# The token-mixing sums of a fused transformer block, moved from VectorE to ScalarE and GpSimd

## The chip, the cores and the metric

The kernel runs on one core of one Trainium2 chip. The metric is the device time of one execution in microseconds (us). The engines are named as in the profile: PE (TensorE, matmuls), PEld (its weight loads), DVE (VectorE), ACT (ScalarE), POOL (GpSimd), SP (SyncE, here the issuer of most DMAs).

## The reference

The input x has 16 batches of 256 tokens and 256 channels, all in fp32. One block of a network is computed for each batch:

```python
x = x + time_mix(norm_mod(attention(x, mask), cond))     # first half
x = x + ffn_fp4(rotate(x))                               # second half
```

- `attention` has 16 heads of 16 channels, a mask over keys, and an output projection. Its result is normalized by its root mean square, multiplied by a gain and shifted; gain and shift come from the batch's conditioning vector.
- `time_mix` shifts half of the channels by one token (`xx`), and makes three mixtures, which are what this change is about:

```python
xk = x * mix_k + xx * (1.0 - mix_k)      # and xv, xr with mix_v, mix_r
k, v, r = xk @ Wk.T, xv @ Wv.T, xr @ Wr.T
out = (sigmoid(r) * wkv_scan(decay, first, k, v)) @ Wo.T
```

Here x stands for the normalized, modulated attention output. Only the lower 128 channels are shifted, so only they need mixing; for the upper 128 channels xx equals x, and the three mixtures are all x itself.
- `rotate` is a rotation of the channels by quaternions. `ffn_fp4` is a gated feed-forward layer with 704 hidden units, whose inputs and weights are rounded to a 4-bit float format in blocks of 16.

## The kernel before

Channels lie on the 128 partitions (two halves of 128 channels), tokens along the free dimension. A batch is therefore a tile of 128 x 2 x 256. The work of a batch is cut into stages, each a Python generator that emits a few instructions for one or more engines and then yields:

- `ask` (a): the q, k and v projections; from batch 2 on, q and k are split in two parts on POOL (L698) and spread by DMA (SP)
- `attend` (t): scores (L771, L763 for the first two batches), exponentials on ACT (L781, tile `w`), `values` (L793), division
- `leave` (l), eight steps: the output projection, the sum of squares on ACT (L841), `rstd` on POOL (L847, L848), scaling (L851), transposes of the normalized rows into a PSUM bank called `pn` (L656), the shifted lower half `xx` (L863), the upper half `xh` (L871), and the `xx` parts of the three mixtures (L876, tiles `mx`)
- `mix` (m): the three mixtures of the lower half are finished on DVE (L888). Then the k, v and r projections with the weights `ak`, `av`, `ar` (all L632), exponentials (L905, L907, L931), scans and the division. Its last step is a product on POOL (L939)
- `rotate` (r): output projection `ao`, rotation (L965, in the last three batches L956), and the first quantization
- `hidden` (h, i for the two token halves): the gate and up projections (L1005, L1018), activation, quantization (L553 to L563)
- `turn_h` (d, e): transposes of the quantized rows (L608)
- `down` (f): the down projection (L1087, L1094; in the last three batches L1067, L1070) and the output DMA
- beside these, stages for loading and preparing weights, among them R (the rotation, whose POOL scalings are L463 and L468) and W, V (quantizing the weights, L536 to L544)

Nothing in the file decides the order at run time. The string `ORDER` lists 1852 steps by hand-written name and batch (m0 is the next step of `mix` for batch 0, tf of `attend` for batch 15), and the kernel runs through it, so that the instructions of a step are appended to each engine's queue. An engine runs its queue strictly in that order and waits at each instruction until its inputs are there and its output buffer is free. PE thus works on several batches in turn, which fills its waits. A second string, `BANKS`, gives the PSUM bank (0 to 7) for each bank request in that order.

In the part that is changed: the mixture tile of k, for instance, is `mx["k"]`. `leave` writes into it (1 - mix_k) * xx plus the shift of the own part, on ACT. `mix` then reads the own x out of the bank `pn`, multiplies it by the gain of k, and adds the tile, in one DVE instruction. The bank `pn` is thus held until the third of these DVE instructions is done.

Of the kernel before, what the change touches and what calls it, by code (L numbers as in the profile page):

```python
# [8 lines left out]
F32 = mybir.dt.float32  # L9
# [4 lines left out]
AF = mybir.ActivationFunctionType  # L14
ALU = mybir.AluOpType
# [3 lines left out]
P = 128  # L19
# [12 lines left out]
a2 R l0 a2 M W0 l0 V0 W0 W3 l0 W5 M A t1 W3 A t1 l0 W2 t1 T a3 R l0 l0 a2 m0 l0 a3 l1 A l1 W0 m0 m0 R W1 m0 m0  # L32
m0 m0 m0 a2 l1 a2 m0 l1 t2 W5 V0 R t2 t2 t2 a3 m0 V1 m0 m0 t2 t2 m0 W3 l1 t2 W3 m0 l1 m0 t2 t2 t2 t2 R t2 t2 t2
R m0 V0 t2 W0 W0 l1 m1 a3 W4 a3 a3 m0 V0 W3 l1 t2 m1 W3 a3 t2 t2 W2 W2 W0 A m1 m1 l2 A m1 m1 W4 l2 r0 m1 l2 m1
l2 r0 a4 a3 m1 m1 l2 l2 m1 V1 m1 l2 a3 W2 m1 a3 t3 m2 W2 m1 t3 m1 t3 r0 t3 t3 a4 m1 t3 t3 l2 m2 a5 m2 t3 t3 r0
a4 m2 t3 t3 a4 t3 m2 t3 m1 a4 r0 m2 t3 m2 t3 a4 r0 r0 t3 r1 m2 a4 t3 m2 r1 a5 t3 r0 r1 a4 r1 r0 m2 m2 r0 r1 V1
V1 m2 a4 m2 a5 l3 r1 m2 a4 l3 l3 r1 i0 a5 i0 m2 V1 t4 i0 a4 t4 V1 i0 V1 i0 h0 t4 i0 r1 i0 t4 h0 h0 a5 t4 h0 t4
t4 l3 m2 t4 t4 i0 r1 i0 t4 t4 t4 t4 l3 t4 V1 a5 h0 i0 l3 t4 m2 r1 a5 i0 a5 l3 t4 l3 m3 e0 h0 t4 m3 r2 m3 a5 a5
V1 m3 i0 i0 m3 t4 r2 m3 a6 m3 m3 a6 a5 m3 a5 m3 l4 m3 e0 m3 l4 a6 m3 m3 a6 h0 t5 i0 t5 t5 m3 i1 a6 t5 m3 t5 h0
t5 i1 l4 i1 l4 t5 i1 t5 t5 t5 r2 t5 m3 t5 i1 t5 a6 l4 t5 a6 i0 t5 r2 r2 a7 i1 t5 e0 t5 a6 i1 l4 h0 h1 l4 d0 h0  # L40
m4 t5 h1 r3 h0 e0 r2 h1 h1 l5 h0 r3 l4 a7 r2 a6 m4 h1 l5 l5 h0 m4 a6 i1 m4 l5 a6 h0 a7 m4 r2 a6 m4 h1 d0 a7 m4
i1 m4 t6 e1 i1 h1 h1 r2 i1 e1 t6 t6 a7 m4 i1 m4 r2 m4 t6 d1 m4 m4 t6 t6 m4 m4 t6 t6 d1 t6 i1 t6 l5 h0 h2 t6 i1
i1 a8 t6 m4 t6 d0 l5 l5 h2 t6 h2 a7 h2 e1 a7 m5 l5 i2 d0 r3 e1 a7 a7 a7 h2 r3 a7 i2 r3 t6 i2 m5 i2 a7 m4 f0 f0
i2 r3 r3 i2 i2 h2 h1 m5 h1 r4 h2 h1 h2 f0 f0 t7 t7 f0 r4 t6 t7 t7 a8 d2 m5 t7 h1 t7 d2 h1 r3 a8 h1 m5 r3 m5 t6
t7 m5 h1 m5 t6 i2 t7 a8 t7 d1 h2 t7 t7 t7 t7 h2 e2 d1 h2 a8 t7 l6 l6 h2 m5 a8 l6 a8 m5 m5 l6 t7 l6 r4 a8 m5 h2
m5 e2 m5 r3 r4 i2 r4 l6 a8 i2 h2 a8 l6 h2 f1 a8 i3 m5 i2 r4 i3 m6 i3 a8 l6 m5 r4 i2 m6 a9 f1 m5 m6 i3 f1 i2 t8
t8 t8 f1 i2 t7 t8 d2 f1 t8 t8 i2 r5 t7 t8 t7 r5 d2 a9 t8 t8 a9 t8 t8 i3 m6 a9 a9 m6 t8 t8 i3 m6 i3 aa a9 m6 t8
e2 l7 m6 l7 a9 m6 m6 i3 h3 m6 i3 a9 l7 m6 h3 h3 h3 i3 l7 i3 i3 t8 e3 h3 h3 m6 e2 a9 h3 m6 h3 h3 e3 a9 i3 a9 f2
m6 i3 r4 f2 f1 h3 f2 a9 t9 t8 i3 t9 r4 t9 m6 t9 h3 f0 f2 t9 t9 f2 m6 e3 h3 r6 h3 r4 t9 t8 r6 h3 t8 t9 e3 t9 l7
d3 t9 aa d3 r5 aa t9 l7 l7 l7 i4 i4 t9 i4 h3 r5 r5 m7 r5 m7 aa i4 t9 d3 aa m7 m7 r5 t9 h4 ab m7 l8 i4 m7 m7 i4  # L50
h4 l8 i4 aa aa m7 m7 h4 d3 h4 h4 i4 m7 aa aa e4 i4 h4 m7 m7 l8 m7 i4 l8 t9 f3 l8 m7 i4 l8 l8 h4 h4 m7 d4 m7 h4
m7 i4 aa aa h4 f2 m8 h4 f3 h4 l8 i4 m8 i4 m8 aa r7 d4 h4 f3 e4 r5 i4 f3 ta h4 ta t9 f3 ta r7 h4 ta d4 ab ta t9
r7 ta ab r7 ab r7 ac ta d4 t9 ta ta r7 r7 r6 ta r6 m8 ab ta ta ta m8 m8 e4 ta r6 ab m8 m8 e4 m8 ab ab r5 m8 l9
ab ab r5 h5 m8 f3 h5 m8 i5 r6 h5 r6 i5 h5 l9 i5 h5 m8 h5 i5 ta i5 h5 l9 h5 m8 ab l9 h5 m8 i5 ab i5 tb r6 h5 tb
tb h5 r6 i5 h5 ta tb tb r6 e5 h5 f4 ta f4 m8 h5 ta tb m8 tb tb e5 tb tb f4 f4 d5 tb l9 l9 f4 r8 i5 l9 h5 tb d5
d5 r8 l9 r8 ac m9 m9 m9 r8 m9 m9 la r7 i5 r8 la r8 m9 h6 ad i5 i5 d5 r7 la r8 ac i5 h6 h6 ac i5 tb m9 i5 la h6
m9 e5 r7 m9 e5 ac la ac tb h6 ac m9 r8 la m9 h6 h6 la ma m9 ac m9 i6 m9 i6 m9 i6 h6 la ac ac i7 i6 ma d6 i6 ac
ma i6 i7 i7 m9 m9 h7 i7 tb ac i7 i7 d6 i6 h7 f5 i7 f5 h7 h7 i6 tc f4 tc tc i7 f5 tb tc h7 f5 h7 h7 f5 r9 r9 h6
tb i6 tc ad h6 h7 i6 tc e6 ad h6 ad h6 h6 r8 i6 tb h6 ad tc e6 tc tc tc ma tc ma i6 ma tc r8 tc tc e7 e7 ma h7
h6 h7 tc ma r9 r9 ad h7 i6 ad i7 ma r9 i7 ad h7 i7 ma h7 i6 lb ad r9 h7 i7 h8 ma lb ma i7 i6 ad lb d6 h8 e6 lb  # L60
lb r9 d6 lb h8 e6 lb ad r9 ma i7 h8 ma h8 mb ma f6 ad h8 td h8 ma tc h8 td td h7 lb td mb td f6 tc mb td r9 td
ae tc ma td td f6 d7 td i7 td mb mb d7 td mb r9 f6 i8 f6 ra i8 mb mb i8 td ra td e7 td ra d8 i8 ae i8 mb ae ra
e7 ra i8 ae ra td i8 mb d7 ra td ae ae i9 i9 mb lc i8 i9 i9 mb i9 lc i8 i9 ae lc f6 i8 ae ra ae mb ae ae lc lc
mb td i8 h8 f5 d7 i9 f7 lc h8 i8 h9 mb mb lc ae h8 h9 lc mc h8 mc i8 f7 i8 h8 h9 mb f7 h8 h9 mc h9 d8 f7 f7 te
te i8 rb mc te h9 rb h9 mc h9 mc rb te te af e8 te rb ra rb mc mc rb ld ld ld rb mc te ld mc te te i9 e8 te ld
i9 mc h8 ld i9 ra mc rb ld af te af i9 mc mc h9 te i9 md te i9 mc i9 af h9 e8 i9 te ld rb te af e9 mc h9 rb md
e9 md af te af e9 d8 md te h9 mc md te md af C md ia af d8 ia h9 md md ha ia ia md e8 ha ia f8 f8 e9 ha ia md f8
md ha ia tf tf h9 tf d9 d9 f8 md md ha md ia tf af tf af rc ia f8 ha md tf ia ha ia rc tf tf tf ia tf rc tf ib
rc tf tf ib ib ha tf ib da ia tf rc h9 f7 da tf rc ib d9 ia ib ea le tf hb le ib le ea tf le ha hb ia rc hb ha
ea ib le ib ha hb ha d9 hb le ea ha le rc le eb ha lf me ib me f9 ib hb md me lf me me hb rc ib me ib me hb me  # L70
ib rc hb hb f9 db f9 ha hb da me f9 db lf rd hb me lf hb ib lf hc eb hb da f9 me me rd eb hc lf hc hc f8 rd hb
lf me mf hc fa rd hc rd fa lf fa me hc rd mf me rd f9 mf db mf db hc dc mf rd ic fa mf rd me fa ic ic ic mf ic
rd dc me hc eb ic re hc mf re mf ic fb ic re ic hc re ic ec mf hc fb fb ic re hc hc hc ic ec mf mf mf dc id dc
ic mf re ic mf re ic id id fb id ec mf ec id re fc re hd fb mf fc id id id hd rf id re hd hd rf ed hd rf he id
rf ed ie rf hd hd id ie fc ie rf hd rf id rf dd hd ie dd hd hd rf id rf id hd he he he id ed hd hd ie if fa if
if hd ed if dd ie he dd fd he ie fd ie if he fd ie ee ie ie fd ee he he if hf if de hf he he de ie ie if ef fb
ef if he hf ie ie he he if hf ff ee ee he if hf de de if fd fe hf hf if hf hf hf hf fe hf hf if hf fe fc C df if
fe hf df ef ef fc fc df df ff ff ff ff C ff fe C ff
"""


BANKS = """
0123456701 2345670512 3470512364 7130526471 0357264135 7260413574 2603475045 3751062475 1062437504 2635704260
3425601734 2015437205 4736024173 5641735026 4137520417 4520734152 6451723451 7452374213 5062143502 1346703124
6031276352 1620127430 6052743052 4763021475 6210521547 1023564237 5062375041 2630741256 0754160253 4172501672
5416071254 6721540732 6732015432 7163721543 7215640713 5762145302 6170327604 5171423064 5273014562 7410367451
0324537426 3415073621 5076231540 6357402617 3520465731 7047230416 5027341237 4560523174 3026134027 1324601257
0263417264 5172451706 4570164235 7140235712 6352023167 0251473561 2473061247 0563270146 5702465724 3647023574
6125476152 4316705416 0753640756 2473651023 4673570214 3657234673 0536217430 1353671462 5013453125 2320452052
1023424510 5103210  # L90
"""


# [1 line left out]
def kernel(  # L95
# [28 lines left out]
    nc = tc.nc  # L124
    B, S, E = x.shape
# [15 lines left out]
    wk = ctx.enter_context(tc.tile_pool(name="work", bufs=1))  # L141
# [12 lines left out]
    def ps():  # L154
        return bank("ps")
# [141 lines left out]
    gain_of = const.tile([P, 3, NB], F32, tag="gain_of", name="gain_of")  # L297
    shift_of = const.tile([P, 3, NB], F32, tag="shift_of", name="shift_of")
    rest_of = const.tile([P, 3], F32, tag="rest_of", name="rest_of")
# [364 lines left out]
    xTs, qks, oTs, xns, ys, x1s, xqs, hqs = {}, {}, {}, {}, {}, {}, {}, {}  # L664
# [168 lines left out]
    def leave(b):  # L833
# [21 lines left out]
        pn = ps()  # L855
        transpose_all(pn, rn_)
        yield
        xx = xx_lo[b % 2]
# [6 lines left out]
            )  # L865
        yield

        mx = {}
        xns[b] = (mx, pn)
        mx["h"] = wk.tile([P, S], F32, tag="xh", name="xh", bufs=2)  # L870
        nc.scalar.activation(  # L871
            mx["h"], pn[:, S : 2 * S], AF.Identity, bias=shift[:, 1, b : b + 1], scale=gain[:, 1, b : b + 1]
        )
        for i, nm in enumerate("kvr"):
            mx[nm] = wk.tile([P, S], F32, tag="mx" + nm, name="mx")
            nc.scalar.activation(  # L876
                mx[nm], xx, AF.Identity, bias=shift_of[:, i, b : b + 1], scale=rest_of[:, i : i + 1]
            )
            if i == 0:
                yield  # L880
        yield


    def mix(b):
        mx, pn = xns.pop(b)

        for i, nm in enumerate("kvr"):
            nc.vector.scalar_tensor_tensor(  # L888
                mx[nm], pn[:, 0:S], gain_of[:, i, b : b + 1], mx[nm], ALU.mult, ALU.add
            )  # L890
            yield
        ek = wk.tile([P, E2, S], F32, tag="ek", name="ek")
        sa, sb = a_sum[b % 2], b_sum[b % 2]
# [243 lines left out]
    def exact(b, mask_b, v_pad, sl):  # L1137
# [82 lines left out]
        nc.vector.tensor_mul(flat(oT), flat(un), pd)  # L1220
        oTs[b] = oT
        yield from leave(b)

    ok = nc.values_load(within, min_val=0, max_val=1)
# [52 lines left out]
```

## Time and profile before

| what | before |
|---|---|
| median of 3 runs | 644.36 us (644.35 to 644.53) |
| the profiled execution's own time | 643.86 us |
| its span, first to last instruction | 642.1 us |
| granted TensorE clock, mean | 0.998 |
| last matmul ends at | 635.5 us |
| DMA moved | 57.71 MB, 90 GB/s |

A row of the groups reads: line, engine, operation, output tile and input tiles, shapes, count, then the busy time in us, the mean ns of one, and the engine's idle time before them with what ended it. A row of a timeline reads: start in us, duration in us, engine, line, operation, tiles, count; an idle time of the engine before it stands in brackets with what ended it. For TensorE one matmul of fp32 data is recorded as two rows, and a busy time includes the time in its pipeline, so that two matmuls that follow each other overlap in the records.

### The profile page before, as it was taken

How to read it: one execution, taken by the hardware profiler on the slowest of the kernel's cores; microseconds unless marked ns; L12 is line 12 of the kernel's file. 1: busy time of each engine (PE TensorE's matmuls, PEld its weight loads, DVE VectorE, ACT ScalarE, POOL GpSimd, SP SyncE). 2: the span in 40 equal slices, each digit the busy share in tenths (PEclk: the TensorE clock that was granted, in tenths of full speed). 3: DMA queues.
4: the chain of work that ended last, by engine and by line, in shares of the span. 5: the costliest groups of instructions: out<-in, count | busy, mean ns of one | idle time of the engine just before them, and what ended most of it. 6: DMA issues, size and time to landing. Idle time of an engine off the chain costs nothing.

```text
span 642.1 us, 11016 instructions
## 1 busy us (share of the span) xinstructions
PE 632.5 (99%) x3808; PEld 451.4 (70%) x3808; DVE 575.8 (90%) x1178; ACT 389.5 (61%) x903; POOL 161.6 (25%) x214
## 2 busy tenths in 40 slices
PE   9999999999999999999999999999999999999995
PEld 7568877676766777767767667767776667776674
DVE  6997899888988887999999999999999999999993
ACT  3879793866866565666665646754684665432442
POOL 3353213230313212222122321313131122212221
PEclk9999999999999999999999999999999999999999
DMA  6643524333341425233330322304305100000011
GB/s 169 172 149 120 165 83 132 132 116 117 115 136 61 147 51 174 69 103 115 124 107 17 132 83 93 122 1 125 106 33 174 25 2 16 17 1 1 2 32 55
DMA packets 62847, 57.71 MB, mean 90 GB/s; under 512 B 36912, under 2 KB 40896, under 8 KB 62784
## 3 DMA queue, kind: packets, MB, share of 16 engines
q1 hardware_dynamic: 62416, 56.65, 29.1%
q8 instruction: 32, 0.52, 0.3%
q10 hardware_dynamic: 368, 0.28, 0.1%
q14 instruction: 31, 0.25, 0.1%
HBM read 38.03 MB, written 18.87 MB: 89 GB/s over the span
## 4 chain that ended last, share of the span: by engine, by line
PE 82%; DVE 12%; ACT 2%; issue 2%; DMA 1%; SPq 0%; POOL 0%; DVEq 0%
PE ps L632 24%; PE ps L1005 14%; PE ps L793 9%; PE ps L644 7%; PE ps L1087 7%; PE pss L771 5%; PE ps L1018 5%; PE ps L608 3%; PE ps L965 2%; PE pss L763 2%; DVE v L561 1%; DVE am L553 1%; PE ps L656 1%; DVE ps L1034 1%; DVE th L1032 1%
## 5 line engine op out<-in xcount | busy, mean ns | idle before, releaser
L781 ACT ACTIVATE w<-pss 128x512 f32<-128x512 f32 x256 | 133.3, 611 | 48.7 <-PE pss L771 44.7
L1005 PE MATMUL ps<-guT,xqT 128*128 128x512 f32 x256 | 117.9, 594 | 0.1
L563 POOL TENSOR_TENSOR hq<-v,am 128x192 f32<-128x192 f32 (+1 forms) x64 | 50.1, 786 | 197.1 <-DVE v L561 177.6
L1005 PEld LDWEIGHTS ps<-guT,xqT 128*128 128x128 f32 x256 | 47.1, 190 | 42.3 <-issue 37.3
L698 POOL TENSOR_TENSOR two<-two 128x512 f32<-128x512 f32 x28 | 35.7, 1275 | 119.8 <-ACT two L691 85.2
L793 PE MATMUL ps<-w,v_one 128*32 128x256 f32 x1024 | 62.7, 382 | 0.3
L558 ACT ACTIVATE m<-ps 128x192 bf16<-128x192 f32 (+1 forms) x64 | 29.8, 467 | 49.7 <-DVE ps L556 49.3
L1087 PE MATMUL ps<-hT,downT 128*128 128x256 f32 x260 | 59.5, 379 | 0.0
L1087 PEld LDWEIGHTS ps<-hT,downT 128*128 128x128 f32 x260 | 49.1, 190 | 9.8 <-issue 2.2
L1030 ACT ACTIVATE th<-ps 128x192 f32<-128x192 f32 (+1 forms) x64 | 29.7, 467 | 40.0 <-PE ps L1005 20.5
L936 DVE RECIPROCAL den<-den 128x512 f32<-128x512 f32 x16 | 53.4, 3337 | 0.1
L793 PEld LDWEIGHTS ps<-w,v_one 128*32 128x32 f32 x1024 | 31.9, 109 | 25.9 <-ACT w L781 5.5
L771 PEld LDWEIGHTS pss<-qT,kT 64*128 64x128 f32 x448 | 30.6, 185 | 22.8 <-issue 10.6
L1018 PE MATMUL ps<-guT,xqT 128*128 128x384 f32 x128 | 46.6, 488 | 0.0
L771 PE MATMUL pss<-qT,kT 64*128 64x256 f32 x448 | 42.0, 306 | 0.1
L561 DVE SCALAR_TENSOR_TENSOR v<-m,ps 128x192 f32<-128x192 bf16 (+1 forms) x64 | 33.3, 521 | 4.5 <-POOL hq L563 0.5
L560 DVE SCALAR_TENSOR_TENSOR ps<-m,ps 128x192 f32<-128x192 bf16 (+1 forms) x64 | 33.2, 519 | 4.0 <-ACT m L558 3.9
L556 DVE SCALAR_TENSOR_TENSOR ps<-ps,rs 128x192 f32<-128x192 f32 (+1 forms) x64 | 34.1, 533 | 2.2
L608 PE MATMUL ps<-ident,hq 128*128 128x128 f32 (+1 forms) x204 | 34.7, 282 | 1.2 <-POOL hq L563 1.2
L608 PEld LDWEIGHTS ps<-ident,hq 128*128 128x128 f32 (+1 forms) x204 | 22.5, 135 | 18.3 <-issue 7.5
L1032 DVE SCALAR_TENSOR_TENSOR th<-th,ps 128x192 f32<-128x192 f32 (+1 forms) x64 | 32.1, 506 | 3.0 <-ACT th L1030 2.9
L1034 DVE SCALAR_TENSOR_TENSOR ps<-th,ps 128x192 f32<-128x192 f32 (+1 forms) x64 | 33.2, 518 | 1.2 <-PE ps L1005 0.2
(203 smaller groups left out, 1340.8 us busy)
## 6 DMA issues: line engine op xcount, KB each, us to landing
kept<-two SPq DMA_DIRECT2D x28, 512.0 KB, 2.8
qT<-kept SPq DMA_DIRECT2D x112, 128.0 KB, 2.9
kT<-kept SPq DMA_DIRECT2D x112, 128.0 KB, 2.8
x_sb<-in_x_dram SPq DMA_DIRECT2D x64, 64.0 KB, 2.4
out_dram<-o_sb SPq DMA_DIRECT2D x52, 64.0 KB, 1.9
out_dram<-o_sb SPq DMA_DIRECT2D x6, 128.0 KB, 1.7
raw<-in_L_ffn_w_down_dram SPq DMA_DIRECT2D x2, 352.0 KB, 3.8
raw<-in_L_ffn_w_gate_dram SPq DMA_DIRECT2D x5, 128.0 KB, 3.2
```

The lines of the kernel that those rows point to most:

```text
L561: nc.vector.scalar_tensor_tensor(v, m, BASE, x, ALU.max, ALU.subtract)
L563: nc.gpsimd.tensor_tensor(blk(dst), blk(v), bc(am), ALU.mult)
L608: nc.tensor.transpose(pt[0:n, (k - k0) * P : (k - k0 + 1) * P], src[:, k * P : k * P + n], ident)
L632: nc.tensor.matmul(pool_tile[:, ot * n : (ot + 1) * n], w[:, ct, ot * P : (ot + 1) * P], src[ct], start=(ct == 0), stop=(ct == E2 - 1),)
L644: nc.tensor.matmul(pool_tile[:, tt * E : (tt + 1) * E], srcT[:, ct, tt * P : (tt + 1) * P], w[:, ct, :], start=(ct == 0), stop=(ct == E2 - 1),
L771: nc.tensor.matmul(quad[2 * s + r][:, i * S : (i + 1) * S], kT[rows_, 2 * r + i, g, ks], qT[rows_, 2 * r + i, g, :], start=True, stop=True,)
L781: nc.scalar.activation(w[kt][:, r].rearrange("p i q -> p (i q)"), quad[r], AF.Exp)
L793: nc.tensor.matmul(pu[32 * r : 32 * r + 32, i * S : (i + 1) * S], vo[:, kt, 8 * g + 2 * r + i, :], w[kt][:, r, i, :], start=(kt == 0), sto ...
L936: nc.vector.reciprocal(flat(den), flat(den))
L1005: nc.tensor.matmul(p_[:, 0:n], xqT[:, ct, tt * P : (tt + 1) * P], guT[:, ct, base : base + n], start=(ct == 0), stop=(ct == E2 - 1),)
L1018: nc.tensor.matmul(p_[:, 0 : 2 * n].rearrange("p (u f) -> p u f", u=2), xqT[:, ct, tt * P : (tt + 1) * P], guT[:, ct, :].rearrange("p (u f ...
L1087: nc.tensor.matmul(pdn[:, 0:S], downT[:, k, h * P : (h + 1) * P], hT[:, k, :], start=(k == 0), stop=False)
```

## The change

Three things are done. First, ACT now makes both parts of a mixture, each in a tile of its own: the own part (gain times `pn` plus shift) in a new tile `own`, of which there are two buffers for the three parts k, v and r; and the rest, (1 - mix) * xx, in `mx`, now without the shift. Second, the addition is done by POOL, from two tiles on the chip; DVE has no part in it, and `pn` is read by ACT alone. Third, the first 250 of the 1852 steps in `ORDER` stay, and all behind them are put in a new order, with a new `BANKS`. The steps themselves are the same ones, apart from what the first two points change in them. Two of the kernel's helper stages (the fallback behind the check at the end, which does not run here) use the same functions. From line 889 on, a line of the new file has a number one lower than in the old one.

```diff
@@ -32,62 +32,62 @@
 m0 m0 m0 a2 l1 a2 m0 l1 t2 W5 V0 R t2 t2 t2 a3 m0 V1 m0 m0 t2 t2 m0 W3 l1 t2 W3 m0 l1 m0 t2 t2 t2 t2 R t2 t2 t2
 R m0 V0 t2 W0 W0 l1 m1 a3 W4 a3 a3 m0 V0 W3 l1 t2 m1 W3 a3 t2 t2 W2 W2 W0 A m1 m1 l2 A m1 m1 W4 l2 r0 m1 l2 m1
-l2 r0 a4 a3 m1 m1 l2 l2 m1 V1 m1 l2 a3 W2 m1 a3 t3 m2 W2 m1 t3 m1 t3 r0 t3 t3 a4 m1 t3 t3 l2 m2 a5 m2 t3 t3 r0
...
+l2 r0 a4 a3 m1 m1 l2 l2 m1 l2 r0 m1 m2 m1 W2 r0 a3 r0 m1 l2 a3 t3 t3 t3 m2 m1 m2 m2 t3 m1 r0 a4 r0 m1 a5 r0 t3
...
@@ -865,29 +865,28 @@
-        mx = {}
-        xns[b] = (mx, pn)
+        mx, own = {}, {}
+        xns[b] = (mx, own)
         mx["h"] = wk.tile([P, S], F32, tag="xh", name="xh", bufs=2)
         nc.scalar.activation(
             mx["h"], pn[:, S : 2 * S], AF.Identity, bias=shift[:, 1, b : b + 1], scale=gain[:, 1, b : b + 1]
         )
         for i, nm in enumerate("kvr"):
+            own[nm] = wk.tile([P, S], F32, tag="own", name="own", bufs=2)
+            nc.scalar.activation(
+                own[nm], pn[:, 0:S], AF.Identity, bias=shift_of[:, i, b : b + 1], scale=gain_of[:, i, b : b + 1]
+            )
             mx[nm] = wk.tile([P, S], F32, tag="mx" + nm, name="mx")
-            nc.scalar.activation(
-                mx[nm], xx, AF.Identity, bias=shift_of[:, i, b : b + 1], scale=rest_of[:, i : i + 1]
-            )
+            nc.scalar.activation(mx[nm], xx, AF.Identity, scale=rest_of[:, i : i + 1])
             if i == 0:
                 yield
         yield


     def mix(b):
-        mx, pn = xns.pop(b)
-
-        for i, nm in enumerate("kvr"):
-            nc.vector.scalar_tensor_tensor(
-                mx[nm], pn[:, 0:S], gain_of[:, i, b : b + 1], mx[nm], ALU.mult, ALU.add
-            )
+        mx, own = xns.pop(b)
+        for nm in "kvr":
+            nc.gpsimd.tensor_tensor(mx[nm], own[nm], mx[nm], ALU.add)
             yield
```

## The prediction

> **What bounds the kernel now.** I read the page's busy times first, then the engines' table by stretches of 8 us, then the timelines of PE and ACT where that table shows an engine without a gap.
>
> ```profile
> PE 632.5 (99%) x3808; PEld 451.4 (70%) x3808; DVE 575.8 (90%) x1178; ACT 389.5 (61%) x903; POOL 161.6 (25%) x214
> ```
>
> PE is busy 99% of the span. A busy PE need not be at its pace, so I compared starts with starts. A projection of four matmuls recurs every 1.73 us, a `values` group of 16 (L793) every 1.86 us, four 128x512 records every 1.72 us. Taking each kind of group at its shortest repetition, all the matmuls need some 615 us; the delays over that pace are 15 us in the whole run. Of these about 9 us are the same 0.09 us again and again, where the array changes from full height to 64 rows or 32 columns (169 such changes in the order before, 170 in the order after). The rest of the span is a start of 6.5 us before the first projection and 6.6 us after the last matmul (635.5 us). So waits for data on PE come to about 5 us, and this is all that a relieved VectorE can give back. In the last quarter DVE is nearly as full as PE (57.6 of 60 us between 500 and 560), but PE does not stand there.
>
> Where does PE depend on ACT?
>
> ```profile
> core 0: us, PE busy (x) PEld busy (x) DVE busy (x) ACT busy (x) POOL busy (x), PEclk, DMA share, GB/s
> 44.00:52.00 8.00, 8.00 (x67) 6.38 (x66) 6.93 (x26) 6.81 (x16) 6.07 (x18) 1.00 0.52 174
> 52.00:60.00 8.00, 7.90 (x51) 6.33 (x53) 5.93 (x12) 8.00 (x22) 2.16 (x3) 1.00 0.49 159
> ```
>
> Between 52 and 60 us ACT is busy 8.00 of 8.00: it is the bound of that stretch. Its timeline:
>
> ```profile
> 48.64 0.56 ACT L871 ACTIVATE xh<-ps,shift,gain 128x256 f32<-128x256 f32 x1
> 49.10 1.57 ACT L876 ACTIVATE mx<-xx_lo,shift_of,rest_of 128x256 f32<-128x256 f32 x3
> 50.58 0.58 ACT L690 ACTIVATE two<-ps 128x512 fp32r<-128x512 f32 x1
> ...
> 56.40 4.03 ACT L781 ACTIVATE w<-pss 128x512 f32<-128x512 f32 x8
> 60.23 0.68 ACT L931 ACTIVATE ps<-ps 128x512 f32<-128x512 f32 x1
> ```
>
> No row from 48.64 to 60.75 has an idle time before it. The eight exponentials of `w` end at 60.4 us, and PE needs the last of them:
>
> ```profile
> 48.86 1.89 PE L644 MATMUL ps<-wt_o,oT 128*128 128x256 f32 x8
> 50.59 0.59 PE L632 MATMUL ps<-mx,wt_ak 128*128 128x256 f32 x2
> ...
> 59.90 2.06 PE L793 MATMUL ps<-w,v_one 128*32 128x256 f32 x32
> 61.89 0.74 PE L771 MATMUL pss<-qT,kT 64*128 64x256 f32 x8
> ...
> 68.00 1.93 PE L793 MATMUL ps<-w,v_one 128*32 128x256 f32 x32
> 69.86 0.66 PE L333 MATMUL ps<-ident,yT 128*128 128x128 f32 x4
> ```
>
> The `values` group at 59.90 takes 1.99 us to the next start, the one at 68.00 takes 1.86. The difference is PE waiting for ACT: there is no slack here. The first 250 steps of the order, which stay as they are, reach to about 78 us and hold the mixing of batches 0 and 1.
>
> **The change part by part.** The rows for its pieces:
>
> ```profile
> L888 DVE SCALAR_TENSOR_TENSOR mx<-ps,gain_of,mx 128x256 f32<-128x256 f32 x48 | 22.1, 471 | 4.4 <-ACT mx L876 4.3
> L871 ACT ACTIVATE xh<-ps,shift,gain 128x256 f32<-128x256 f32 x16 | 9.0, 564 | 0.4
> L698 POOL TENSOR_TENSOR two<-two 128x512 f32<-128x512 f32 x28 | 35.7, 1275 | 119.8 <-ACT two L691 85.2 <-issue 26.6 <-DVE rs L555 7.8
> ```
>
> DVE loses 48 instructions, 22.1 us: 576 becomes 554. ACT gains 48 reads of a PSUM bank, each like L871. From its start to the next start that one takes 0.46 us (48.64 to 49.10), so 48 x 0.46 = 22 us: 390 becomes 412. The other part stays (L876 recurs each 0.49 us; dropping its bias changes no size). POOL gains 48 adds of 128x256. The nearest row is L698, two full fp32 inputs of SBUF, 1.275 us for 512 columns. Half is 0.64; scaling the 128x256 multiply with a broadcast input (0.62 us) by 1275/1060, the two kinds at 512, gives 0.75. I take 0.70, so 34 us: 162 becomes 195, 30%.
>
> Against this stands the Trainium skill, GPSIMD Engine Reference, "Engine selection": elementwise work with two inputs belongs on VectorE, GpSimd being about twice as slow. The row agrees on the slowness (0.70 against 0.47), but by it POOL has 480 us free. By the rule each mix pays 0.23 us three times, 11 us in all, if the adds were on the path; by the rows they are not, as soon as the order leaves room. From the transposes of `pn` (L656) to the first `ak` matmul the new order has between 5.9 and 40 us of PE work in batches 1 to 15. The chain in between (shift 1.1, `xh` 0.5, own 0.5, rest 0.6, add 0.7: 3.4 us) fits. In batch 0 it is 3.5 us from the transposes' end to L632, and there it does not.
>
> Batch 0, worked out (with each engine's instructions in the new order): own k at 49.10, rest k 49.56 to 50.16, the add on POOL 50.2 to 50.9. On POOL the eight rotation scalings that used to run until 50.2 now stand behind the three adds; they end near 55.2 and are needed at 56.3, and `rstd` follows at 55.9, before ACT asks for it. PE asks for the k sum at 50.59 and gets it at 50.95: 0.4 us of wait. Own r reuses own k's buffer (two for three parts), so it waits for the k add, 50.95; ACT would reach it at 51.0, so this wait costs nothing here. L690 then starts at 52.0 in place of 50.58: ACT is 3 x 0.47 = 1.4 us late, has no idle time to absorb it, and the last exponential ends at 61.8. PE's `values` group, come at 60.3, goes on at 61.8, and the next group starts 1.2 to 1.4 us late; the 0.4 lies inside this. Bounds: 1.2, and 2.1 if the k add is held up. For that second bound: SBUF — State Buffer, "Who interferes with whom", says that a VectorE instruction with two SBUF inputs and a GpSimd read exclude each other. L540 and L541 (two SBUF inputs, 0.69 us each) stand at 50.1 here; no row has one beside an add. I take 1.3, since L888 no longer stands before them and they can run earlier.
>
> Batch 1: own k delays ACT by 0.46, with 0.15 us of idle before L690 at 67.69; own v and r add 0.95; the idle 0.68 before `ek` at 72.28 takes most of it. 0.6 us reaches `rnorm` at 74.01, and 0.2 of it the transposes at 77.27. Range 0 to 0.5. Together the kept prefix costs 1.5 us (1.2 to 2.6).
>
> Behind step 250 the order is new on every engine. Summing rows over the new order, DVE has 0 to 7 us less work per 100 us of PE, ACT 2 to 5 more (at most 75 of 100), POOL 3 to 7 more; DVE is again the fullest (97 of 100 from 300 to 400 us and after 500), and none exceeds PE. PE's own work and its mode changes are equal. What was waited for there is about 4 us, nearly 2 of it at the very end:
>
> ```profile
> 628.27 0.60 PE L608 MATMUL ps<-ident,hq 128*128 128x128 f32 x4
> 629.58 0.55 PE L608 MATMUL ps<-ident,hq 128*128 128x128 f32 x3 [0.70 <-POOL hq L563]
> 630.66 0.44 PE L608 MATMUL ps<-ident,hq 128*128 128x128 f32 x2 [0.54 <-POOL hq L563]
> ```
>
> PE waits there for the last hidden rows to come through DVE and POOL. Before: 3.0 us of down projection stands between the last L1018 and these transposes; in the new order 5.6 us. That can hide up to 1.7 us. On the other side, a new order brings new collisions: own r behind the k add in all 16 batches, with hq or yT multiplies that wait for DVE queued ahead on POOL in most of them, and behind own r on ACT the exponentials that PE needs. I set these against each other: -0.1. SP issues the same DMAs in a new order; they have slack before (no DMA holds PE after 6 us).
>
> **Sum.** Span 642.1 + 1.5 - 0.1 = 643.5. The profiled execution took 643.86, 1.8 more than its span, and the median of the runs is 644.36, 0.5 above that; 644.36 + 1.4 = 645.8.
>
> **The rivals.** (1) Prefix cost alone, as above: 645.8, 38%. (2) The end gives it back: the 2.6 us of extra cover take away the 1.7 us of waits, and the prefix costs 1.5: 644.2, no measurable change, 35%. For it: the longer cover; against: DVE is full before it, so the last rows may simply come later. (3) Faster, not slower: DVE's 22 us matter wherever PE waits for DVE or POOL; end -1.7, half of the 2 us of other waits -1, prefix at its least 1.2: 644.36 - 1.5 = 642.9. It decides if the exponentials at 56.4 start less than 1 us late. Since PE's waits are only 5 us in all, it can hardly give more; 15%. (4) The two-buffer ring: own r stands on ACT for the k add while POOL waits for DVE, 0.5 us in each of the 14 later batches where ACT then is late for `w`, tanh or abs: with half of it passed on to PE 3.5 us, 649.3, 12%. For it: POOL's queue waits for DVE 178 us in front of hq; against: ACT is at most 75% full there.
>
> 0.2% (1.3 us) is about what a measurement of this kernel tells from no change. Faster 15%, same 35%, slower 50%. The range 643.0 to 649.0 leaves out half of (3) and the upper half of (4); the likeliest case alone is 645.4 to 647.0.
>
> **What would show it.** After: L690 near 52.0, `values` near 60.3 with 3 us to the next start; ACT 8.00 of 8.00 there; own about 0.56 each, adds about 0.70; no change in PE's count; the waits at 628 shorter. Wrong if PE's starts at 62 us are where they were, or if PE shows stops of over 0.3 us between 100 and 600 us.

## The result, and the profile after

| | before | after |
|---|---|---|
| median, beside each other on one chip (19 runs each) | 644.53 us | 645.61 us |
| ratio to before, 95% interval | 1 | 1.0015 (1.0008 to 1.0022) |
| the same on a second chip (57 and 22 runs) | 645.90 us | 646.11 us; 1.0013 (1.0003 to 1.0023) |
| the profiled execution's own time, span | 643.86, 642.1 us | 645.88, 644.1 us |
| last matmul of any size starts at | 635.27 us | 637.26 us |

One of the 22 executions on the second chip (731.85 us, at a clock of 0.85) was in the slow state, and the ratio leaves it out. The kernel is about 1 us slower (0.5 to 1.4 us by the first interval, 0.2 to 1.5 by the second), just what a measurement can tell. First the page's busy times after:

```profile
PE 634.2 (98%) x3808; PEld 451.7 (70%) x3808; DVE 563.5 (87%) x1130; ACT 408.2 (63%) x951; POOL 195.8 (30%) x262
```

DVE fell from 575.8 to 563.5, ACT rose from 389.5 to 408.2, POOL from 161.6 to 195.8; PE's count did not change. The groups of the new instructions:

```profile
L889 POOL TENSOR_TENSOR mx<-own,mx 128x256 f32<-128x256 f32 x48 | 34.8, 728 | 45.8 <-ACT mx L880 44.8
L876 ACT ACTIVATE own<-ps,shift_of,gain_of 128x256 f32<-128x256 f32 x48 | 27.1, 564 | 1.6 <-POOL mx L889 1.6
L880 ACT ACTIVATE mx<-xx_lo,rest_of 128x256 f32<-128x256 f32 x48 | 24.4, 508 | 0.2 <-PE ps L632 0.2
```

The add takes 0.73 us and the own part 0.56. The rows show an idle time of 1.6 us in all before the own part, waiting for POOL. The stretch from 52 to 60 us in the table by stretches:

```profile
core 0: us, PE busy (x) PEld busy (x) DVE busy (x) ACT busy (x) POOL busy (x), PEclk, DMA share, GB/s
52.00:60.00 8.00, 7.56 (x42) 6.07 (x41) 4.08 (x8) 7.99 (x22) 5.33 (x13) 1.00 0.54 174
```

ACT is full, as before (the fourth busy time, 7.99 of 8), and POOL's 2.16 of 8 has become 5.33. The timelines of PE, ACT and POOL in this stretch:

```profile
44.69 1.93 PE L793 MATMUL ps<-w,v_one 128*32 128x256 f32 x32
...
51.26 0.70 PE L632 MATMUL ps<-mx,wt_ak 128*128 128x256 f32 x2 [0.16 <-POOL mx L889]
...
56.64 0.61 PE L771 MATMUL pss<-qT,kT 64*128 64x256 f32 x5
57.50 1.64 PE L771 MATMUL pss<-qT,kT 64*128 64x256 f32 x11 [0.25 <-ACT rnorm L851]
...
61.55 1.99 PE L793 MATMUL ps<-w,v_one 128*32 128x256 f32 x32
63.47 0.75 PE L771 MATMUL pss<-qT,kT 64*128 64x256 f32 x8
```

```profile
52.10 0.58 ACT L690 ACTIVATE two<-ps 128x512 fp32r<-128x512 f32 x1
...
55.71 0.89 ACT L748 ACTIVATE v_one<-ps,keep 128x256 f32<-128x256 f32 x2
56.61 0.84 ACT L851 ACTIVATE rnorm<-ps,rstd 128x256 f32<-128x256 f32 x2
```

```profile
50.48 1.57 POOL L889 TENSOR_TENSOR mx<-own,mx 128x256 f32<-128x256 f32 x2 [2.53 <-ACT mx L880]
52.28 0.72 POOL L889 TENSOR_TENSOR mx<-own,mx 128x256 f32<-128x256 f32 x1 [0.22 <-ACT mx L880]
...
55.11 0.37 POOL L468 TENSOR_SCALAR x1T<-ident,cols 64x64 f32<-64x64 f32 x1
55.57 0.22 POOL L847 TENSOR_SCALAR ms<-ms 128x2 f32<-128x2 f32 x1
55.87 0.71 POOL L848 TENSOR_TENSOR rstd<-ms,mhalf 128x2 f32<-128x2 f32 x1
```

The `values` group at 44.69 stood at 44.34 before, and nothing changed lies ahead of it: the first loads came a little later in this execution. Such shifts of the start, up to 2.8 us between two executions, enter before 12 us and are carried on to the end; this, more than the kernels, spreads the times. So from here on I measure from the start of this group: **A** to the next `values` group (batch 0), **T** to the start of the last matmul (L510). Before: A = 59.90 - 44.34 = 15.56, T = 635.27 - 44.34 = 590.93. After: A = 16.86, T = 592.57. So batch 0 costs 1.30, and everything behind it 0.34 in this execution (0.00 in a second one, below). At the end PE no longer waits (before, 0.70 and 0.54 us at these transposes):

```profile
626.29 2.76 PE L1066 MATMUL ps<-downT,hT 128*128 128x256 f32 x12
628.88 0.61 PE L1069 MATMUL ps<-ident,x1T 128*128 128x128 f32 x4
629.33 2.32 PE L1066 MATMUL ps<-downT,hT 128*128 128x256 f32 x10
631.49 1.38 PE L608 MATMUL ps<-ident,hq 128*128 128x128 f32 x9
```

### The profile page after: what moved, and what is told of

It reads as the page before. It is cut to its first block, busy times and chain, and to the rows that moved or that the text cites. A ratio compares the mean times of both kernels' runs of the same rounds, so it can differ in the third digit from the quotient of the medians.

```text
span 644.1 us, 11082 instructions
## 1 busy us (share of the span) xinstructions
PE 634.2 (98%) x3808; PEld 451.7 (70%) x3808; DVE 563.5 (87%) x1130; ACT 408.2 (63%) x951; POOL 195.8 (30%) x262
## 4 chain that ended last, share of the span: by engine, by line
PE 85%; DVE 9%; ACT 3%; issue 1%; POOL 1%; DMA 1%; SPq 0%; DVEq 0%; POOLq 0%
PE ps L632 23%; PE ps L1004 14%; PE ps L793 9%; PE ps L644 7%; PE ps L1086 7%; PE ps L1017 6%; PE pss L771 5%; PE ps L608 4%; PE ps L1066 2%; PE ps L964 2%; PE pss L763 2%; PE ps L656 1%; DVE den L935 1%; DVE v L561 1%; PE ps L1093 1%
## 5 line engine op out<-in xcount | busy, mean ns | idle before, releaser
L563 POOL TENSOR_TENSOR hq<-v,am 128x512 f32<-128x512 f32 (+1 forms) x64 | 50.1, 785 | 160.9 <-DVE v L561 149.2
L558 ACT ACTIVATE m<-ps 128x512 bf16<-128x512 f32 (+1 forms) x64 | 29.8, 466 | 60.7 <-DVE ps L556 60.6
L698 POOL TENSOR_TENSOR two<-two 128x512 f32<-128x512 f32 x28 | 35.6, 1271 | 86.9 <-ACT two L691 44.5
L1029 ACT ACTIVATE th<-ps 128x512 f32<-128x512 f32 (+1 forms) x64 | 29.6, 466 | 38.4 <-PE ps L1004 27.0
L889 POOL TENSOR_TENSOR mx<-own,mx 128x256 f32<-128x256 f32 x48 | 34.8, 728 | 45.8 <-ACT mx L880 44.8
L1031 DVE SCALAR_TENSOR_TENSOR th<-th,ps 128x512 f32<-128x512 f32 (+1 forms) x64 | 32.3, 507 | 10.5 <-ACT th L1029 10.5
L561 DVE SCALAR_TENSOR_TENSOR v<-m,ps 128x512 f32<-128x512 bf16 (+1 forms) x64 | 33.3, 521 | 4.6
L556 DVE SCALAR_TENSOR_TENSOR ps<-ps,rs 128x512 f32<-128x512 f32 (+1 forms) x64 | 34.1, 533 | 2.2
L560 DVE SCALAR_TENSOR_TENSOR ps<-m,ps 128x512 f32<-128x512 bf16 (+1 forms) x64 | 33.2, 518 | 3.1 <-ACT m L558 2.7
L1033 DVE SCALAR_TENSOR_TENSOR ps<-th,ps 128x512 f32<-128x512 f32 (+1 forms) x64 | 33.2, 519 | 2.9 <-PE ps L1004 1.7
```

The source lines that it names most:

```text
L561: nc.vector.scalar_tensor_tensor(v, m, BASE, x, ALU.max, ALU.subtract)
L563: nc.gpsimd.tensor_tensor(blk(dst), blk(v), bc(am), ALU.mult)
```

## The experiments

The theories: **1**, ACT, with three more instructions in batch 0 of the kept prefix, makes PE late there, and the new order behind step 250 nets about nothing. **Rival A** (not the interval A), the new order is the cost. **B**, DVE's relief is what pays later. **C**, the POOL add ahead of `ak` is the cost. **D**, the new instructions need the new order. The **ring** of two own tiles. Two were added for the end: E1 (the place of the last down projections gives back the waits there) and E2 (DVE's lighter load does). All twelve kernels, with A and T as above ("rest" is T - A, before 575.37) and the ratio to the kernel before on the same chip:

| kernel | A | rest | T against before | ratio, 95% interval |
|---|---|---|---|---|
| after, a second time | 16.87 | 575.37 | +1.31 | 1.0013 (1.0003 to 1.0023) |
| after, batches 0 and 1 mixed as before | 15.78 | 575.77 | +0.62 | 1.0012 (1.0000 to 1.0024) |
| before, 3 more ACT reads in batch 0 | 17.53 | 575.37 | +1.97 | 1.0035 (1.0023 to 1.0046) |
| new instructions, old order | 16.85 | 584.55 | +10.47 | 1.0163 (1.0140 to 1.0186) |
| after, all adds on DVE | 16.61 | 593.69 | +19.37 | 1.0289 (1.0263 to 1.0315) |
| after, three own tiles | 16.76 | 575.65 | +1.48 | 1.0016 (1.0007 to 1.0025) |
| after, batch 0's adds on DVE | 16.61 | 575.73 | +1.41 | 1.0025 (1.0015 to 1.0035) |
| after, 11 batches mixed as before | 15.79 | 598.38 | +23.24 | 1.0324 (1.0301 to 1.0346) |
| before, tail of the new order | 15.56 | 575.38 | +0.01 | 1.0001 (0.9993 to 1.0009) |
| after, tail of the old order | 16.85 | 575.40 | +1.32 | 1.0028 (1.0018 to 1.0037) |
| after, two copies on DVE | 17.21 | 575.48 | +1.76 | 1.0036 (1.0022 to 1.0049) |
| before, that tail and two copies on DVE | 15.57 | 575.02 | -0.34 | 0.9997 (0.9989 to 1.0006) |

The two profiled executions of the kernel after agree within 0.01 us in A and differ by 0.34 in the rest. Each row rests on one profiled execution; that of "11 batches" is the slowest of its five runs (671.41 us, median 667.10), so that its T is some 4 us above the usual.

**Batch 0: taking the change out of the prefix.**

```diff
+            if b < 2:
+                own[nm] = pn
...
```

The same test stands at the addition, which DVE makes from the bank where b < 2.

> The kernel after, in its order and with its banks, but batches 0 and 1 mixed as before (the own part read from the bank and added by DVE, ACT makes only the xx part). Theory 1 (three more ACT instructions in batch 0 of the kept prefix cost 1.2 us, the new order behind it about nothing): 1.2 us below the kernel after, 644.4, equal to the kernel before; L690 of batch 0 back at 50.6 to 51.0 us and no wait at the first L771 behind 57 us. Rival A (the new order behind step 250 costs it): equal to the kernel after, 645.6. Rival C (only the slower POOL add ahead of the first ak costs, 0.3 us): 645.3.

A falls by 1.08 to 15.78, of the 1.30 that it had gained; L690 is back at 51.00 and the score group is whole. So the cost lies in batch 0, in the size of theory 1, and rival A in its strict form falls. But the edit takes away ACT's own parts and POOL's adds at once, and does not tell these two apart. The last 0.2 stay open: PE's v projection starts 0.15 us late (at 52.88), and no wait shows why. T falls by 1.02 against the first execution of after and 0.69 against the second. The medians alone do not tell the two kernels apart.

**Batch 0: adding the ACT work to the kernel before.**

```diff
+            for _ in range(1 if b == 0 else 0):
+                own = wk.tile([P, S], F32, tag="own", name="own", bufs=2)
+                nc.scalar.activation(
+                    own, pn[:, 0:S], AF.Identity, bias=shift_of[:, i, b : b + 1], scale=gain_of[:, i, b : b + 1]
+                )
```

> The kernel before, with three more ACT instructions in batch 0 alone: the own part of each mixture is also written by ACT into a tile that nobody reads; DVE goes on mixing from the bank. Order and banks are those of before. Theory 1 (ACT has no slack from 49 to 60 us): 3 x 0.46 = 1.4 us later on ACT, 1.1 to 1.4 us longer, 645.7, with L690 near 52.0 us. Rival A (the new order costs it) and rival C (the POOL add costs it): as before, 644.5, no change over 0.2 us.

The two rows of ACT and PE that say most:

```profile
52.64 0.57 ACT L877 ACTIVATE own<-ps,shift_of,gain_of 128x256 f32<-128x256 f32 x1 [0.55 <-DVE mx L893]
```

```profile
55.66 1.99 PE L644 MATMUL ps<-wt_v,xT 128*128 128x256 f32 x8 [1.01 <-ACT two L691]
```

More than expected: +1.97. ACT's own v had to wait 0.55 us, because DVE reads the same bank here and the program makes the two readers take turns (DVE's next reading waited 0.25 us for ACT's own r, with which it shares only the bank). At L690 ACT is 2.02 us later than before, measured from the same landmark ((54.54 - 46.28) - (50.58 - 44.34)), and this becomes 1.97 on PE, and then nothing more to the end. So ACT's lateness is passed on nearly one to one, without POOL having any part in it.

**Batch 0: which engine?** In the first kernel here the three adds of batch 0 go to DVE and ACT keeps both parts; in the second, ACT is relieved of two copies (r weights, a part of the gate weights) and POOL keeps the adds.

```diff
-            nc.gpsimd.tensor_tensor(mx[nm], own[nm], mx[nm], ALU.add)
+            (nc.vector if b < 1 else nc.gpsimd).tensor_tensor(mx[nm], own[nm], mx[nm], ALU.add)
```

> The kernel after, but the three additions of batch 0 stand on DVE; ACT still makes both parts. Theory 1 (three more ACT instructions cost the 1.2 us in batch 0): as the kernel after within 0.4 us, with the values group still 1.2 us late against its pace. Rival C (the slower POOL add costs it): 0.4 to 1.2 us below the kernel after.

```diff
-            if name in ("q", "k", "v", "o"):
+            if name in ("q", "k", "v", "o", "ar"):
-        nc.scalar.copy(guT[...], pt[...])
+        copy = nc.vector.tensor_copy if j == 2 * P else nc.scalar.copy
+        copy(guT[...], pt[...])
```

> The kernel after with two copies out of a bank in batch 0's stretch (the weights of the r projection, and one quarter of the gate weights) moved from ACT to DVE, which stands idle for 2 us there. Theory 1 (ACT is the bound from 49 to 60 us, one to one): ACT is 0.94 us earlier there, and the interval from the values group at 44.6 us to the one at 61.5 falls from 16.86 to 15.9 to 16.0 us, the whole by 0.9 us, to the level of the kernel before. Rival C (POOL's add or another wait sets it): 16.6 or more.

With the adds on DVE, A is 16.61: ACT alone still costs 1.05, and POOL has 0.25 of the 1.30. With all 48 adds on DVE (below) A is 16.61 again. With ACT relieved, 15.9 to 16.0 was expected, and A rose to 17.21. Theory 1 in its simple form fails here. ACT's, POOL's and PE's timelines of that kernel:

```profile
51.49 0.56 ACT L877 ACTIVATE own<-ps,shift_of,gain_of 128x256 f32<-128x256 f32 x1 [0.34 <-POOL mx L890]
...
53.66 0.40 ACT L842 ACTIVATE rnorm<-ps 128x256 f32<-128x256 f32 x1
...
56.85 0.84 ACT L852 ACTIVATE rnorm<-ps,rstd 128x256 f32<-128x256 f32 x2 [0.75 <-POOL rstd L849]
```

```profile
50.38 1.76 POOL L890 TENSOR_TENSOR mx<-own,mx 128x256 f32<-128x256 f32 x2 [2.54 <-ACT mx L881]
52.52 0.73 POOL L890 TENSOR_TENSOR mx<-own,mx 128x256 f32<-128x256 f32 x1 [0.39 <-ACT mx L881]
...
55.36 0.37 POOL L468 TENSOR_SCALAR x1T<-ident,cols 64x64 f32<-64x64 f32 x1
55.81 0.22 POOL L848 TENSOR_SCALAR ms<-ms 128x2 f32<-128x2 f32 x1
56.11 0.71 POOL L849 TENSOR_TENSOR rstd<-ms,mhalf 128x2 f32<-128x2 f32 x1
```

```profile
51.51 0.70 PE L633 MATMUL ps<-mx,wt_ak 128*128 128x256 f32 x2 [0.51 <-POOL mx L890]
```

ACT is at the scaling (L852) early, and stands there 0.75 us for `rstd`, which POOL makes only behind three adds and eight rotation scalings. L852 starts 0.03 us after `rstd` ends (56.11 + 0.71 = 56.82, and 56.85). Look back at the rows of after: there `rstd` ends at 55.87 + 0.71 = 56.58, and ACT's scaling starts at 56.61, again 0.03 behind it. So POOL holds ACT up in the kernel after too, though no idle time stands in that row. By its own queue ACT would have come earlier. From the two `v_one` (L748) to the scaling it takes 0.73 us before and 0.71 with batch 0's adds on DVE, where `rstd` is there in time, as two ACT instructions overlap in the records; in after it takes 56.61 - 55.71 = 0.90. The rows of before, and of the kernel with batch 0's adds on DVE:

```profile
54.24 0.84 ACT L748 ACTIVATE v_one<-ps,keep 128x256 f32<-128x256 f32 x2
54.97 0.84 ACT L851 ACTIVATE rnorm<-ps,rstd 128x256 f32<-128x256 f32 x2
```

```profile
58.04 0.90 ACT L748 ACTIVATE v_one<-ps,keep 128x256 f32<-128x256 f32 x2
58.75 0.92 ACT L851 ACTIVATE rnorm<-ps,rstd 128x256 f32<-128x256 f32 x2
```

So batch 0 is late for two reasons that lie side by side. ACT's own parts alone make 1.05. POOL's adds, with ACT relieved, still make the whole delay, and in after they are the later of the two: `rstd` comes 0.18 behind ACT's own queue, and the k add, as the next run shows, holds own r up by 0.10. So taking away the adds alone gives 0.25, taking 0.94 off ACT alone gives nothing, and taking away both gives 1.08. That A even rose by 0.35 is the work of one slow k add (1.08 us, see the last section): by it own r waits 0.34 us, PE 0.51 in place of 0.16, and `rstd` ends 12.24 us behind the landmark in place of 11.89. Without it A would be about 16.86, an estimate from these rows.

**The ring of own tiles.**

```diff
-            own[nm] = wk.tile([P, S], F32, tag="own", name="own", bufs=2)
+            own[nm] = wk.tile([P, S], F32, tag="own", name="own", bufs=3)
```

> The kernel after with three buffers for the own tiles, so that own r need not wait for the k add (a small one-time tile of the test in batch 2 moves into that ring to make room). Theory 1 (this ring costs nothing, since own r waited once in 48): equal to the kernel after within 0.5 us. Ring rival: 1 us or more below the kernel after.

The kernel after beside it:

> The kernel after, unchanged, beside the next three on the same chip, so that they can be set against it directly. All theories: 1.0 to 1.2 us above the kernel before.

T differs by 0.17, and the ratios overlap nearly whole. But A, which repeats within 0.01, is 16.76 in place of 16.87: with two tiles own r starts 0.49 us behind the rest of v (50.75 to 51.24 in after), behind the k add, and with three 0.40. So the ring has 0.10 us of batch 0's cost, and nothing measurable of what lies behind it (575.65, between the two executions of after).

**Behind step 250: the new instructions in the old order.** The order and the banks are those of before, the code that of after. One of the five small moves:

```diff
-l3 m3
+m3 l3
```

> The new instructions (own part on ACT, add on POOL) in all batches, with the order and the banks of before; only in batches 3, 7, 9, 12 and 14 the last step of leave moves behind the k add, by 1 to 8 steps, since two own tiles serve three parts. Theory 1 (prefix +1.2, later batches have slack on ACT and POOL): 645.7 to 646.5, about the kernel after. Rival A (the new order itself is the cost): as before or faster, 644.5 or less. Rival D (the longer chain of own, rest and add stands right ahead of ak in the old order and needs the new order to be hidden): over 647, with waits of L632 for POOL's add in more than ten batches.

A is 16.85, exactly that of after; but the rest is 9.18 us longer. D holds, and theory 1's 645.7 to 646.5 does not, though D's waits were expected at the wrong place: the line of L632 waits for the add only 0.5 us. The largest stop, in the timelines of POOL, SP's DMA queue and PE, all of this kernel (its line numbers are one lower than those of after):

```profile
128.64 1.58 POOL L888 TENSOR_TENSOR mx<-own,mx 128x256 f32<-128x256 f32 x2 [5.91 <-ACT mx L879]
130.44 0.73 POOL L888 TENSOR_TENSOR mx<-own,mx 128x256 f32<-128x256 f32 x1 [0.22 <-ACT mx L879]
131.12 1.28 POOL L697 TENSOR_TENSOR two<-two 128x512 f32<-128x512 f32 x1
```

```profile
132.42 0.37 SPq L703 DMA_DIRECT2D kept<-two  x1
135.18 5.00 SPq L707 DMA_DIRECT2D kT<-kept  x8
```

```profile
140.18 0.38 PE L770 MATMUL pss<-qT,kT 64*128 64x256 f32 x1
142.41 0.71 PE L770 MATMUL pss<-qT,kT 64*128 64x256 f32 x7 [1.85 <-DMA kT<-kept]
143.05 3.01 PE L1003 MATMUL ps<-guT,xqT 128*128 128x512 f32 x4
145.98 1.22 PE L770 MATMUL pss<-qT,kT 64*128 64x256 f32 x8
```

The subtraction that splits k (L697, in before L698) has its two inputs, but stands on POOL behind three adds that wait for ACT. Before it starts at 124.68, its DMA at 125.98 and the eight DMAs of kT at 128.84; here they start at 131.12, 132.42 and 135.18. The start shift and the delays so far account for 2.6 us of it. PE finds the scores' kT missing and stops for 1.85 us. Then comes a second price: the same matmuls run slowly, four 128x512 records in 2.93 us instead of 1.72. The stop and this are some 3.5 of the 9.2 us; stops of 1.47 and 1.07 us at 284.8 and 308.2 us bring it to 6.1, and the remainder was not followed up one by one. The table by stretches shows the clock (the column ahead of the DMA share):

```profile
142.00:144.00 2.00, 1.59 (x9) 1.02 (x10) 2.00 (x1) 1.17 (x3) 1.95 (x2) 0.97 0.47 106
144.00:146.00 2.00, 2.00 (x5) 0.36 (x3) 1.03 (x1) 0.89 (x2) 1.83 (x4) 0.50 0.69 254
146.00:148.00 2.00, 2.00 (x11) 1.45 (x11) 0.00 (x0) 1.19 (x3) 1.14 (x2) 0.68 0.02 8
```

**Behind step 250: the adds on DVE, in the new order.**

```diff
-            nc.gpsimd.tensor_tensor(mx[nm], own[nm], mx[nm], ALU.add)
+            nc.vector.tensor_tensor(mx[nm], own[nm], mx[nm], ALU.add)
```

> The kernel after with one thing changed: the 48 additions stand on DVE instead of POOL, so that DVE gets about 16 to 22 us back (0.33 to 0.47 each). Theory 1 (DVE's time is not what PE waits for; prefix cost unchanged, since ACT is unchanged): 645.6, within 0.7 us of the kernel after. Rival B (DVE's relief is what pays in the second half, 1.6 us, and hides the cost of the change): 647 or more. Rival C (the POOL add is what is late at the first ak): 645.3 or less.

Theory 1 as it stood ("within 0.7 us") fails by far, and B in its mild form too: the rest is 18.3 us longer. DVE's busy time is 580.0, hardly more than the 575.8 with which the kernel before runs in 644 us. So it is not the amount. DVE's waits in this kernel, and PE's:

```profile
DVE mx L889 <- ACT mx L880: 8.7, 11, 3.2
```

```profile
PE ps L608 <- POOL hq L563: 5.4, 3, 2.5
PE ps L632 <- DVE u L803: 2.9, 1, 2.9
```

The new order puts the adds where ACT has not finished its parts; on POOL that wait (45.8 us in the group's row of after) mostly holds up nothing, on DVE 8.7 us of it stand ahead of the quantization and the division that PE needs.

**Behind step 250: the old mixing in the new order.** It was put into 11 of the 16 batches. All 16 were not tried: in batches 6, 7, 8, 10 and 11 the new order gives the bank away before DVE would have read it, and the queues would wait for each other in a circle.

```diff
-            if b < 2:
+            if b in (0, 1, 2, 3, 4, 5, 9, 12, 13, 14, 15):
```

> The kernel after in its new order, but batches 0 to 5, 9 and 12 to 15 (11 of 16) mixed as before: own part read from the bank by DVE, only the xx part on ACT. Theory 1 as it stands after the first four runs (what DVE does in the new order matters only by where its instructions stand in the queue; the new order puts the mixing steps early, before ACT's part is ready, since a waiting POOL costs nobody): 5 to 12 us above the kernel after, with DVE waiting for ACT at the mixing, as in the run with all additions on DVE (8.7 us there). Rival A (the new order itself is slower, and the new instructions are what hides it or not at all): within 1.5 us of the kernel after. Rival B' (it is DVE's work, not its place, that counts): 11/16 of 22 us of DVE work comes back, and the time rises in proportion in the second half only, where DVE is full: 2 to 4 us.

A is 15.79, as it must be, and the rest 23.0 us longer. PE's longest wait in it:

```profile
211.16 1.40 PE L771 MATMUL pss<-qT,kT 64*128 64x256 f32 x8 [3.98 <-DVE mx L896]
```

These scores need no mixture. They need a bank, and it is the one from which DVE reads its own part, behind other work. With the own part on ACT that bank is free early, and the new order relies on it. Both rival A (the new order is merely slower) and the smaller sum of B' fall. The size was missed too: 5 to 12 us above after were expected, and the median is 21 above (667.10 against 646.11).

**The end.** The last 28 of the 1852 steps were exchanged between the two orders, with their banks; for the kernel before:

```diff
-fe hf hf if hf fe fc C df if fe hf df ef ef fc fc df df ff ff ff ff C ff fe C ff
+hf if if hf fe hf fc fe fc C df fe df fc fe ef hf df ef df ff ff ff ff C ff ff C
```

> The kernel before with one thing changed: the last 28 steps of the order (from step 1824 on, where both orders have done the same steps) and their banks are those of the kernel after; the mixing is that of before in all batches. Theory E1 (the gain at the end comes from where the last down projections stand, ahead of the last transposes of hidden rows): the two waits of 0.70 and 0.54 us for POOL's hq at 629 and 631 us shrink to 0 to 0.3, and from the values group at 44.3 us to the last matmul it takes 0.6 to 1.2 us less than the 590.9 of before. Rival E2 (the gain at the end comes from DVE's lighter load): 590.9 within 0.2, the same waits.

> The kernel after with the last 28 steps of the order, and their banks, of the kernel before; everything else as after. Theory E1: waits for hq come back, 0.6 to 1.2 us longer than the 592.2 to 592.6 us of after (from the first values group to the last matmul). Rival E2 (DVE's lighter load ends the last rows earlier): no change over 0.3.

Both moved nothing (T +0.01 against before; +1.32, against +1.31 for after a second time). But they decide nothing between E1 and E2: PE's sequence between the last L1018 and the transposes proved to be the same as in the kernel before (and after, respectively), since the steps that set the cover lie ahead of step 1824. So the cut was in the wrong place, and it is not shown whether the longer cover or DVE's lighter load ended those waits.

**A version below both?** The kernel before with that tail and the two copies on DVE.

> The kernel before with the last 28 steps of after's order and with the same two copies on DVE: the version that the runs so far point to. Theory 1: ACT had no slack in batch 0 before the change either, so the two copies save what PE waited there, 0.2 to 0.4 us (interval 15.56 to 15.2 to 15.35 us); with theory E1 another 0.6 to 1.2: 0.8 to 1.6 us below the kernel before, below both kernels. Rivals C and E2: within 0.3 us of the kernel before.

A is 15.57, not 15.2 to 15.35. ACT now has 0.64 us of idle time before `v_one`, which waits for PE's v projection: before the change ACT and PE were even there (`v_one` at 54.24 followed the projection's end at 54.20), so that a relief gains nothing and a load costs its full size. The -0.34 of T comes from one wait for hq at the end that was shorter (0.19 in place of 0.54), and the ratio 0.9997 (0.9989 to 1.0006) is no change. None of the kernels beats the one before.

## Why the prediction was right

The forecast was 1.4 us more (645.8). The medians moved by 1.08 on the first chip, the ratio on the second gives 0.8, and T grew by 1.31 and 1.64. The place and the main cause (ACT in batch 0) were right; that the size came out so near is in part luck, since a part of ACT's load was costed too high and POOL's part, put at nothing, filled the gap. By its steps:

- **ACT's load in batch 0: right in place, its size a little over.** L690 was to stand at 52.0 instead of 50.58, 1.4 later; less the start shift it came 52.10 - 0.35 - 50.58 = 1.17 later, of which the wait of own r ("costs nothing here") is 0.10. The own part recurs each 0.45 us as costed. The term that was off is "dropping its bias changes no size": the rest recurs after 0.40 us instead of 0.49 where nothing holds it up. The Trainium skill (ScalarE: Activation LUTs, "What ACT_TABLE_LOAD costs") states 93 ns for each per-partition pointer operand, which is what these rows show; by it the load would have been costed at 1.42 - 3 x 0.09 = 1.15 us. Over the run 48 x 0.09 = 4 us of it explain why ACT has 408 and not 412.
- **POOL hidden in batch 0: not so.** The prediction had the scalings end near 55.2 and `rstd` come "before ACT asks for it". They ended at 55.48, `rstd` at 56.58, and by its own queue ACT would have asked at 56.43 (55.71 + 0.72). Put at nothing, POOL costs 0.25 of the 1.30. The sum for batch 0, 1.3, is the measured 1.30 because ACT's 1.05 and POOL's 0.25 make it up.
- **The wait for the k sum**: 0.4 predicted, 51.26 - 49.21 - 1.73 = 0.32 measured; it lies inside the rest, as said.
- **Where PE stops: one group early.** The `values` group was to be stretched to 3 us. It took 1.92; the stop came in the score group before it, since ACT's scaling of batch 1 frees a bank that the scores take: 0.90 us there (59.22 - 56.64 against 57.54 - 55.86) and 0.43 before it, behind the k sum. The amount was the same, 1.3 us.
- **Batch 1: 0.2 predicted, nothing measured.** From 61.6 to 78 us after runs at the pace of before.
- **Behind step 250: -0.1 predicted, 0.00 and +0.34 measured; right as a sum, and as a balance.** The 1.24 us of waits at the end are gone (up to 1.7 was said), so new delays in the middle took 1.2 to 1.6 us net. In the profiled execution the largest are five short ones between 80 and 400 us, of 0.3 to 0.7 us each. What the prediction did not see is what stands behind the balance: the new instructions cost 9.2 us there in the old order (POOL's queue ahead of the kT DMAs, banks), more than five times the collisions that it weighed, and the new order takes all of that back.
- **Its signs of being wrong.** PE's starts at 62 us did move (61.89 to 63.47). But the other sign, "stops of over 0.3 us between 100 and 600 us", came once, in both executions of after: 0.33 us at 235.04, at L632 behind DVE's L1099. One such stop is too small a thing to tell the theories apart.
- **DVE** fell by 12 us and not by 22. The 0.47 us of a row overlaps the next: two mixes in a row start 0.40 us apart, which makes 19; and single others were longer (L294 3.1 for 0.6 us, L554 10.4 for 8.7 in sum). As PE does not stand for DVE's work, this moved nothing.

Of the rivals, the ring's 3.5 us are refuted by the run with three tiles (0.10, all in batch 0). "The end gives it back" came half true: the end gave back 1.24, and the middle took it. "Faster" failed since batch 0 is 1.3 us late and no wait in the middle went away for it.

## What to carry to other kernels

Where an engine is full, ask of each other queue that the change loads there whether it is tied with it: a delay with two nearly equal causes shows only one of them in the waits, or none, and taking away one of them gives little or nothing. An idle time that a row doesn't show may still be there where instructions overlap in the records, so compare starts with starts. Measure from a landmark that lies ahead of the first changed instruction; 0.1 us of batch 0 could be told here in single executions, where the medians tell 1 us only as something between 0.2 and 1.5. A hand-made order is worth what its instructions make of it: 9 us of cost and 9 us of gain stood behind a result of zero, and the same work on the engine next door, in the same order, cost 18.

## What the runs showed of the hardware

- After a stop of 1.85 us on PE the granted clock went to 0.50, from about 143.9 to 147.3 us, and the matmuls there cost 1.2 + 0.5 = 1.7 us more; the stop cost almost twice itself. The same came behind stops of 2.89 and 2.49 us (all adds on DVE) and of 3.98, 2.58, 1.95 and 1.56 us (11 batches); stops of 1.47, 1.48 and 1.54 us in these kernels and the old-order one did not do it. What decides between 1.54 and 1.56 is not shown. The Trainium skill (TensorE: Matmul & The Clock Gate, "HAM oscillation — how this bites in real kernels") warns of gaps over some 3.4 us; here half of that was enough. The length of the slow stretch, 3.4 us, agrees with its window of 3.4; behind the stop of 3.98 us it was twice that. With 11 batches the slow stretches are 17 us together, so that at half pace up to 8.5 of its 23 us may be the clock's (an estimate from these lengths).
- One add on POOL took 1.08 us in place of 0.72 to 0.75: the k add of batch 0 in the kernel with two copies on DVE, which lay beside L541 (two SBUF inputs) and one of the copies. The prediction had this as its upper bound for the k add, by the Trainium skill's rule (SBUF — State Buffer, "Who interferes with whom") on a VectorE instruction with two SBUF inputs. In five executions, five overlaps each with L812, which also reads two SBUF tiles, left the add at 0.72 to 0.73 and L812 at 0.42. So the rule does not hold for each such pair, and which part of it counts was not tried.
- The start shift of up to 2.8 us enters at the start: PE's first weights stood at 4.06 us (before) or 4.78 (batch 0's adds on DVE), but most of it comes in the first matmuls behind them. The first projection took 1.73 us to the next in the one (6.61 to 8.34) and 2.88 in the other (8.23 to 11.11). What slows these matmuls is not shown.
